# Mixed key pairs of the maxima spread over two items, with the size taken between two exponentials

## The chip, the cores and the metric

The program runs on one core of one Trainium2 chip. The metric is the device time of one execution in microseconds (us), lower being better. The kernel before took 14402.4 us as the median of three runs (14353.14, 14402.4 and 14412.16 us).

The engines are named as the profile names them: PE is TensorE's matmul, PEld its weight load, ACT ScalarE, DVE VectorE, POOL GpSimd, SP SyncE (here only a queue of DMAs).

## The reference, cut to what matters

There are N = 3327 nodes with 128 features. The first layer is a graph layer with residual and layer norm. The second, which takes nearly all the time, is an attention with 128 heads of 8 components each over all nodes, with the adjacency matrix added to the scores twice:

```python
q = (x @ Wq.T).reshape(d, n, h)          # d = 128 heads, n = 3327 nodes, h = 8
k = (x @ Wk.T).reshape(d, n, h)
v = (x @ Wv.T).reshape(d, n, h)
a = jnp.einsum('dnh,dmh->dnm', q, k) * scale
a = a + spatial_encoding + edge_encoding  # both are adj
a = jax.nn.softmax(a, axis=2)
out = jnp.einsum('dnm,dmh->dnh', a, v)
out = out.reshape(n, h * d)
return out @ Wo.T
```

So 128 matrices of 3327 x 3327 scores are made, and of each row its maximum, the exponentials less that maximum, their sum and their product with v.

The adjacency matrix is sparse, with at most 16 entries used in a row. The kernel therefore computes the dense part without it and adds each node's neighbours in a separate pass; the two are joined at the end.

## The kernel before, in words

**Stages.** Up to 460 us the first layer is computed. Up to about 890 us the queries, keys and values are projected and written to DRAM, the queries and keys split into three bf16 parts each, whose products are put together by stacking 48 rows (`KR`). From then to about 14,150 us the attention runs, and then the last stage joins, normalizes and projects.

**The sums.** The heads are worked on in 32 groups of four (`GH`). For each group the queries come in seven blocks (`BLOCKS`): six of 512 and a last one of 255. For each block a loop over 26 tiles of 128 keys (`t`) makes, for each head, the transposed scores in a PSUM bank `e_ps` (L620, three banks), the exponentials `es` (L630), and, two tiles later, the products with v (L588, function `products`). A step over one `t` has two halves of two heads each. In the last block one bank holds two heads of 255 columns (`per = 2`).

**The maxima.** The exponentials need each query's maximum over the keys. The same scores are made a second time, queries on the partitions, 76 items ahead of the sums. An item (`max_products`, L441) fills two PSUM banks `m` (L447; there are two such pairs) with 1024 keys of one head, and VectorE takes the maximum (L466). For 128 queries and four heads there are 13 items: three for each head, and one for the last 255 keys of all four. A full block has 52 items and 52 halves, so one item goes with each half; in the last block one item goes with each `t`. [...]

**Mixed pairs.** For two heads in four (`MIXED`), the first item's 1024 keys are stored as half sums and half differences of neighbouring keys, 512 of each, since max(a, b) = (a + b)/2 + |a - b|/2. Here ScalarE takes the absolute value of the differences' bank (`size`, L458), and one custom VectorE instruction (L461) adds it to the sums' bank and takes the maximum of 512 instead of 1024. Both banks belong to one item; in ScalarE's queue `size` stands ahead of both exponentials of its half. These keys are made by `mixed_keys` (L252) in the projection stage, are stored in `kk_d`, and are loaded by `load_group` into rows 64 and up of `k_st`.

**What sets the order.** Each engine's queue is in the order in which the Python code emits it. The maxima come from a generator (`maxima`, L375) that the loop over `t` advances between its own matmuls. After a block's maxima, `lowest` (one turn later) reduces them, and `to_queries` (eight turns after that) transposes them and sends them over DRAM into the row of `q_st` that makes the matmul subtract the maximum (L431, L435). All of these DMAs, the loads of groups (L326, issued when the maxima reach block 3 of the group before) and of queries, the stores of results and the traffic of the neighbours' pass are issued in order on SyncE's one queue.

**The neighbours.** A second generator, `beside`, is advanced once in four `t` (`PACE`). It first sorts keys and values by node in 256 steps (`by_node`), then takes 26 tiles of nodes (`neighbours`, L480), mostly on GpSimd: 16 steps for the scores of the neighbours, the maximum over the 16 slots on VectorE (`top`, L534), the exponentials on ScalarE, and 16 steps for the values; 36 steps a tile.

## Time and profile before

| | us |
|---|---|
| median of the runs shown | 14402.4 |
| the profiled execution's own time | 14479.67 |
| its span, first to last instruction | 14478.0 |
| TensorE matmul busy | 13415.7 (93%) |
| ScalarE busy | 12902.2 (89%) |
| VectorE busy | 12606.3 (87%) |
| GpSimd busy | 5379.1 (37%) |
| exponentials L630, 21632 of them | 11403.2 |
| maxima L466, 9152 of them | 10662.9 |
| sizes L458, 1664 of them | 994.2 |

The profile is of one execution, taken by the hardware's profiler. Busy times of instructions that overlap are counted once, so that a group's busy time can be less than its count times its mean. Ends of matmuls are modelled. In the stretch from 12,000 to 12,500 us, which has no neighbours' pass, TensorE is busy for 490.5 us, ScalarE for 481.9 and VectorE for 460.9 of 500.

The chain that ended last is followed back from the last instruction, at each step to what released it; its shares say what the end waited for. An idle time of an engine is put down to the instruction that released it. Times in the timeline are from the span's start.

### The profile page before, as it was taken

How to read it: one execution, taken by the hardware profiler on the slowest of the kernel's cores; microseconds unless marked ns; L12 is line 12 of the kernel's file. 1: busy time of each engine (PE TensorE's matmuls, PEld its weight loads, DVE VectorE, ACT ScalarE, POOL GpSimd, SP SyncE). 2: the span in 40 equal slices, each digit the busy share in tenths (PEclk: the TensorE clock that was granted, in tenths of full speed). 3: DMA queues.
4: the chain of work that ended last, by engine and by line, in shares of the span. 5: the costliest groups of instructions: out<-in, count | busy, mean ns of one | idle time of the engine just before them, and what ended most of it. 6: DMA issues, size and time to landing. Idle time of an engine off the chain costs nothing.

```text
span 14478.0 us, 319633 instructions
## 1 busy us (share of the span) xinstructions
PE 13415.7 (93%) x131844; PEld 3272.9 (23%) x131844; DVE 12606.3 (87%) x14091; ACT 12902.2 (89%) x24068; POOL 5379.1 (37%) x4580
## 2 busy tenths in 40 slices
PE   8559999999998999999999999999989999999995
PEld 3212222222222222222222222222212222222213
DVE  6669999999998999898998899899988889999976
ACT  8539999999998999899999999999989989999982
POOL 0410000006665556565565556655646630000002
PEclk9769999999999999999999999999999999999996
DMA  6963333333454444444445544444344531100103
GB/s 252 160 99 32 29 30 31 30 30 77 73 72 62 72 68 75 69 77 74 69 68 68 73 72 72 76 74 71 68 62 75 73 48 18 18 16 11 19 5 101
DMA packets 2711814, 930.03 MB, mean 64 GB/s; under 512 B 2431635, under 2 KB 2559762, under 8 KB 2703683
## 3 DMA queue, kind: packets, MB, share of 16 engines
q1 hardware_dynamic: 2582147, 411.27, 27.7%
q0 software_dynamic: 124176, 453.33, 11.3%
q10 hardware_dynamic: 4016, 44.88, 0.9%
q8 instruction: 1034, 16.94, 0.5%
q14 instruction: 441, 3.61, 0.1%
HBM read 786.20 MB, written 151.91 MB: 65 GB/s over the span
## 4 chain that ended last, share of the span: by engine, by line
PE 72%; ACT 15%; DVE 4%; issue 3%; DMA 3%; POOL 2%; SPq 1%; another core or an unknown queue 0%; ACTq 0%; DVEq 0%; POOLq 0%
PE o L588 34%; PE m L447 29%; ACT es L630 9%; PE e_ps L620 8%; ACT size L458 5%; DVE mx L466 1%; DMA k_st<-k_d 1%; DVE top L534 1%; POOL more L699 1%; ACT o_sb L597 1%; DVE top_at L153 1%; PE acc L145 1%; DVE top_w L152 1%; DMA kk_d<-both_sb 0%; ACT unread L143 0%
## 5 line engine op out<-in xcount | busy, mean ns | idle before, releaser
L630 ACT ACTIVATE es<-e_ps 128x512 f32<-128x512 f32 x21632 | 11403.2, 604 | 515.4 <-PE e_ps L620 305.8
L466 DVE TENSOR_REDUCE mx<-m 128x1 f32<-128x1024 f32 (+1 forms) x9152 | 10662.9, 1215 | 615.5 <-PE e_ps L620 428.4
L620 PE MATMUL e_ps<-q_st,k_st 50*128 50x512 bf16 (+1 forms) x23296 | 6920.9, 370 | 389.5 <-ACT es L630 136.5
L447 PE MATMUL m<-k_st,q_st 48*128 48x512 bf16 (+1 forms) x23296 | 6623.2, 370 | 230.6 <-DMA q_st<-q_d 118.5
L588 PE MATMUL o<-es,v 128*9 128x256 f32 (+1 forms) x83456 | 6732.5, 394 | 15.9 <-issue 15.9
L421 POOL CAST two<-nm 128x16 bf16<-128x16 f32 (+1 forms) x224 | 43.7, 195 | 6805.6 <-DVE nm L415 6805.6
L447 PEld LDWEIGHTS <-q_st 48*128 48x128 bf16 x23296 | 1442.2, 94 | 4861.4 <-issue 4816.2
L588 PEld LDWEIGHTS o<-es,v 128*9 128x9 f32 x83456 | 1242.4, 88 | 4889.4 <-issue 4881.5
L461 DVE CUSTOM_DVE_ANT_0 larger<-size,m 128x512 f32<-128x512 f32 x1664 | 1143.3, 687 | 736.0 <-ACT size L458 732.5
L620 PEld LDWEIGHTS <-k_st 50*128 50x128 bf16 (+1 forms) x23296 | 1415.5, 96 | 695.1 <-issue 526.0
L458 ACT ACTIVATE size<-m 128x512 f32<-128x512 f32 x1664 | 994.2, 597 | 458.7 <-PE e_ps L620 308.3
L521 POOL TENSOR_TENSOR prod<-qn,near_rows 128x1024 f32<-128x1024 f32 x416 | 985.8, 2370 | 98.9 <-DMA near_rows<-kn_d,near 78.0
L557 POOL TENSOR_TENSOR acc<-acc,prod 128x1024 f32<-128x1024 f32 x390 | 885.0, 2269 | 30.6
L556 POOL TENSOR_TENSOR prod<-near_rows,s 128x1024 f32<-128x1024 f32 x390 | 772.0, 1980 | 11.8 <-DMA near_rows<-vn_d,near 4.8
L523 POOL TENSOR_TENSOR half<-prod 128x512 f32<-128x512 f32 x416 | 530.0, 1274 | 32.6
L490 POOL DMA_INDIRECT near_rows<-kn_d,near x416 | 417.3, 1003 | 109.5 <-issue 57.1
L490 POOL DMA_INDIRECT near_rows<-vn_d,near x416 | 411.8, 990 | 65.1 <-issue 25.0
L145 PE MATMUL acc<-a_t,x 128*128 128x512 f32 (+1 forms) x728 | 305.2, 581 | 65.6 <-DMA a_t<-in_adj_dram 44.1
L525 POOL TENSOR_TENSOR quarter<-half 128x256 f32<-128x256 f32 x416 | 254.5, 612 | 32.6
L540 POOL TENSOR_TENSOR s<-s,gain 128x2048 f32<-128x2048 f32 x26 | 93.8, 3608 | 349.7 <-ACT s L539 349.7
L699 POOL TENSOR_TENSOR more<-n_t,down 128x1152 f32<-128x1152 f32 (+1 forms) x26 | 101.0, 3884 | 276.0 <-ACT down L697 138.4
L145 PEld LDWEIGHTS acc<-a_t,x 128*128 128x128 f32 x728 | 141.2, 196 | 229.3 <-issue 182.5
(151 smaller groups left out, 3441.0 us busy)
## 6 DMA issues: line engine op xcount, KB each, us to landing
q_st<-q_d SPq DMA_DIRECT2D x2304, 32.0 KB
a_t<-in_adj_dram ACTq DMA_DIRECT2D x13, 1663.5 KB
a_t<-in_adj_dram SPq DMA_DIRECT2D x13, 1663.5 KB
a_t<-in_adjt_dram SPq DMA_DIRECT2D x13, 1663.5 KB
a_t<-in_adjt_dram ACTq DMA_DIRECT2D x13, 1663.5 KB
q_d<-wq_sb SPq DMA_DIRECT2D x26, 768.0 KB
k_d<-wk_sb SPq DMA_DIRECT2D x26, 768.0 KB
k_st<-k_d SPq DMA_DIRECT2D x32, 623.8 KB
```

Source lines behind the costliest of these rows:

```text
L145: nc.tensor.matmul(acc[:, b, :w], x0[:, t, :], a_t[:, n0 : n0 + w], start=t == 0, stop=t == NT - 1)
L447: nc.tensor.matmul(m[:, n * step : n * step + width], q[64 : 64 + KR, j, i * P : (i + 1) * P], k[64 : 64 + KR, j, c0 : c0 + width], start= ...
L458: nc.scalar.activation(size, m[:, :NB], AF.Abs)
L461: nc.vector.tensor_tensor_reduce(larger, size, m[:, NB:], scale=1.0, scalar=LOWEST, op0=ALU.add, op1=ALU.max, accum_out=dst)
L466: nc.vector.tensor_reduce(dst, src, axis=AX.X, op=ALU.max)
L490: nc.gpsimd.indirect_dma_start(rows.rearrange("p d h -> p (d h)"), None, table, bass.IndirectOffsetOnAxis(ap=near[:, t, i : i + 1], axis=0))
L521: nc.gpsimd.tensor_mul(prod, qn, kg)
L556: nc.gpsimd.tensor_mul(prod, vg, share)
L557: nc.gpsimd.tensor_add(acc[:, :, :H], acc[:, :, :H], prod)
L588: nc.tensor.matmul(o[32 * j : 32 * j + VW, c : c + w], v4[:pt, j, t, :], e[j][:pt, c : c + w], start=t == 0, stop=t == NT - 1,)
L620: nc.tensor.matmul(bank[:pt, j, :w], k[: KR + 2, j0 + j, t * P : t * P + pt], q[: KR + 2, j0 + j, :w], start=True, stop=True,)
L630: nc.scalar.activation(es[:pt, :, :w], bank[:pt, :, :w], AF.Exp, scale=2.0)
```

## The change

A mixed head's 1024 paired keys and its next 1024 plain keys are spread anew over items. Before, one item held differences and sums, and two items held plain keys. Now the item "size" holds the differences in its first bank and 512 plain keys in its second, the item "sums" holds the sums and 512 plain keys, and a third item 1024 plain keys as before. There are as many items, banks and matmuls as before. VectorE takes a maximum over 512 in the item "size", and in the item "sums" the custom instruction on the first bank and a maximum over 512 on the second. The size is kept in SBUF from one item to the next.

In ScalarE's queue the size now stands between the two exponentials of its half. The loop over `t` gives one item to one half with both its banks, and in the last block makes both banks of four heads together, one item beside them.

The maxima's tile `mx` has five slots for each head instead of four, in two fixed buffers that are filled with the lowest value once.

Paired keys begin at the first whole row of 128 of a head (`paired_from`), so that they are eight rows instead of nine. The keys ahead of that are loaded behind the pairs. `mixed_keys` writes pieces of 1, 2, 4 or 8 rows. `load_group` loads the plain heads whole, the mixed ones in up to four pieces: 33 DMAs for keys in place of 24 for each group (30 for the first group, whose first head begins at a whole row).

The neighbours' maximum over 16 slots, one reduction before, is made by five elementwise maxima in four steps, so that a tile has 40 steps instead of 36.

```diff
@@ -49,6 +49,13 @@
 LEAD = 38
 TURN = 8
 MIXED = (0, 2)
+PAIRED = MW
+SLOTS_MX = 5
+
+
+def paired_from(head):
+
+    return -head * N % D
 
 
 def bank_cuts(width):
@@ -263,13 +270,15 @@
                 for head in range(HEADS):
                     if head % GH not in MIXED:
                         continue
-                    r0 = max(head * N // D, t * P)
-                    r1 = min((head * N + MW - 1) // D + 1, (t + 1) * P)
-                    if r0 < r1:
+                    first = (head * N + paired_from(head)) // D
+                    r0, r1 = max(first, t * P), min(first + PAIRED // D, (t + 1) * P)
+                    while r0 < r1:
+                        n = 1 << (r1 - r0).bit_length() - 1
                         nc.sync.dma_start(
-                            kk_d[:, r0 * D // 2 : r1 * D // 2].rearrange("r (p c) -> p r c", p=r1 - r0),
-                            sb[r0 - t * P : r1 - t * P].rearrange("p s a h c -> p (s a h) c"),
+                            kk_d[:, r0 * D // 2 : (r0 + n) * D // 2].rearrange("r (p c) -> p r c", p=n),
+                            sb[r0 - t * P : r0 - t * P + n].rearrange("p s a h c -> p (s a h) c"),
                         )
+                        r0 += n
 
             for t in range(NT):
                 g = slice(t * P * D, (t + 1) * P * D)
@@ -328,19 +337,22 @@
             heads = k_d[:, g * GH * N : g * GH * N + GH * N]
             for slot, parts in KROWS:
                 src = heads[: H * parts].rearrange("r (j n) -> r j n", j=GH)
-                for base, n0 in ((0, 0), (64, MW)):
-                    r = base + H * slot
-                    nc.sync.dma_start(k[r : r + H * parts, :, n0:N], src[:, :, n0:])
+                nc.sync.dma_start(k[H * slot : H * slot + H * parts, :, :N], src)
+                rows = slice(64 + H * slot, 64 + H * slot + H * parts)
                 for j in range(GH):
                     if j not in MIXED:
-                        nc.sync.dma_start(k[r : r + H * parts, j, :MW], src[:, j, :MW])
+                        nc.sync.dma_start(k[rows, j, :N], src[:, j])
                         continue
-                    at = (g * GH + j) * N // 2
+                    n0 = paired_from(g * GH + j)
+                    at = ((g * GH + j) * N + n0) // 2
                     for s in range(2):
                         nc.sync.dma_start(
-                            k[r : r + H * parts, j, s * NB : (s + 1) * NB],
-                            kk_d[s * PARTS * H : s * PARTS * H + H * parts, at : at + NB],
+                            k[rows, j, s * PAIRED // 2 : (s + 1) * PAIRED // 2],
+                            kk_d[s * PARTS * H : s * PARTS * H + H * parts, at : at + PAIRED // 2],
                         )
+                    if n0:
+                        nc.sync.dma_start(k[rows, j, PAIRED : PAIRED + n0], src[:, j, :n0])
+                    nc.sync.dma_start(k[rows, j, PAIRED + n0 : N], src[:, j, PAIRED + n0 :])
             v4 = load.tile([P, GH, NT, VW], F32, name="v4")
             for j in range(GH):
                 at = (g * GH + j) * N
@@ -372,6 +384,25 @@
             return queries[g, b]
 
 
+        mxs = [fixed.tile([P, NB // P, GH, SLOTS_MX], F32, name=f"mx{i}") for i in range(2)]
+        for mx in mxs:
+            nc.vector.memset(mx, LOWEST)
+
+        def items_of(mx, i):
+
+
+            plain = {
+                j: [([(j, c)], [(j, c + NB)], "all", [mx[:, i, j, c // MW : c // MW + 1]]) for c in range(0, 3 * MW, MW)]
+                for j in range(GH)
+            }
+            for n, j in enumerate(MIXED):
+                at = lambda slot: mx[:, i, j, slot : slot + 1]
+                yield [(j, PAIRED // 2)], [(j, PAIRED)], "size", [at(1)]
+                yield [(j, 0)], [(j, PAIRED + NB)], "sums", [at(0), at(3)]
+                yield plain[j][2]
+                yield from plain[j + 1]
+            yield [(0, 3 * MW), (1, 3 * MW)], [(2, 3 * MW), (3, 3 * MW)], "tails", [mx[:, i, :, SLOTS_MX - 1]]
+
         def maxima():
             for g in range(NG):
                 for b, (n0, w) in enumerate(BLOCKS):
@@ -383,18 +414,14 @@
                         group_of(g + 1)
                     if b + 1 < len(BLOCKS) or g + 1 < NG:
                         queries_of(g + (b + 1) // len(BLOCKS), (b + 1) % len(BLOCKS))
-                    mx = work.tile([P, NB // P, GH, 4], F32, name="mx")
+                    mx = mxs[(g * len(BLOCKS) + b) % 2]
                     for i in range(ntl):
-                        for j in range(GH):
-                            for c in range(3):
-                                yield from turn()
-                                banks = [(j, c * MW), (j, c * MW + NB)]
-                                yield (k, q, i, banks, NB, mx[:, i, j, c : c + 1], c == 0 and j in MIXED)
-                        yield from turn()
-                        yield (k, q, i, [(j, 3 * MW) for j in range(GH)], N - 3 * MW, mx[:, i, :, 3], False)
+                        for item in items_of(mx, i):
+                            turn()
+                            yield (k, q, i, *item)
                     late.append([1, lowest, (g, b, q, mx)])
             for _ in range(TURN + 4):
-                yield from turn()
+                turn()
                 yield None
 
         late = []
@@ -406,7 +433,6 @@
             while late and late[0][0] < 0:
                 _, part, args = late.pop(0)
                 part(*args)
-            return ()
 
         def lowest(g, b, q, mx):
 
@@ -438,32 +464,38 @@
                 chunk.rearrange("a (j n) -> a j n", j=GH)[:, :, :w],
             )
 
-        def max_products(item):
-
-            k, q, i, cols, width, dst, mixed = item
+        sizes = []
+
+        def max_item(item):
+
+            k, q, i, *banks, kind, dst = item
             m = ps_m.tile([P, MW], F32, name="m")
-            step = MW // len(cols)
-            for n, (j, c0) in enumerate(cols[::-1] if mixed else cols):
-                nc.tensor.matmul(
-                    m[:, n * step : n * step + width],
-                    q[64 : 64 + KR, j, i * P : (i + 1) * P],
-                    k[64 : 64 + KR, j, c0 : c0 + width],
-                    start=True,
-                    stop=True,
-                )
-                if n == len(cols) // 2 - 1:
-                    yield
-            if mixed:
-                size = work.tile([P, NB], F32, name="size")
-                nc.scalar.activation(size, m[:, :NB], AF.Abs)
+            tail = N - 3 * MW
+            for n, bank in enumerate(banks):
+                width = NB if len(bank) == 1 else tail
+                for x, (j, c0) in enumerate(bank):
+                    at = n * NB + x * NB // 2
+                    nc.tensor.matmul(
+                        m[:, at : at + width],
+                        q[64 : 64 + KR, j, i * P : (i + 1) * P],
+                        k[64 : 64 + KR, j, c0 : c0 + width],
+                        start=True,
+                        stop=True,
+                    )
                 yield
+            if kind == "size":
+                sizes.append(work.tile([P, NB], F32, name="size"))
+                nc.scalar.activation(sizes[-1], m[:, :NB], AF.Abs)
+            yield
+            if kind == "sums":
                 larger = work.tile([P, NB], F32, name="larger")
                 nc.vector.tensor_tensor_reduce(
-                    larger, size, m[:, NB:], scale=1.0, scalar=LOWEST, op0=ALU.add, op1=ALU.max, accum_out=dst
+                    larger, sizes.pop(0), m[:, :NB], scale=1.0, scalar=LOWEST, op0=ALU.add, op1=ALU.max, accum_out=dst[0]
                 )
-            else:
-                src = m if len(cols) == 2 else m.rearrange("p (n c) -> p n c", c=step)[:, :, :width]
-                nc.vector.tensor_reduce(dst, src, axis=AX.X, op=ALU.max)
+            src = m if kind == "all" else m[:, NB:]
+            if kind == "tails":
+                src = m.rearrange("p (n c) -> p n c", n=GH)[:, :, :tail]
+            nc.vector.tensor_reduce(dst[-1], src, axis=AX.X, op=ALU.max)
             yield
 
         def by_node():
@@ -531,7 +563,15 @@
                 yield
                 acc = side.tile([P, HEADS, CW], F32, name="acc", bufs=2)
                 top = side.tile([P, HEADS], F32, name="top")
-                nc.vector.tensor_reduce(top, s.rearrange("p i d -> p d i"), axis=AX.X, op=ALU.max)
+                m8 = side.tile([P, SLOTS // 2, HEADS], F32, name="prod", bufs=2)
+                for i in (0, 4):
+                    nc.vector.tensor_max(m8[:, i : i + 4], s[:, i : i + 4], s[:, 8 + i : 12 + i])
+                    yield
+                nc.vector.tensor_max(m8[:, :4], m8[:, :4], m8[:, 4:])
+                yield
+                nc.vector.tensor_max(m8[:, :2], m8[:, :2], m8[:, 2:4])
+                nc.vector.tensor_max(top, m8[:, 0], m8[:, 1])
+                yield
                 nc.gpsimd.tensor_copy(acc[:, :, CW - 1], top)
                 nc.gpsimd.tensor_sub(s, s, top[:, None, :].to_broadcast([P, SLOTS, HEADS]))
                 yield
@@ -563,15 +603,14 @@
         beside = (x for stage in (by_node(), neighbours()) for x in stage)
         with tc.manual_schedule(engines={ENG.PE, ENG.Activation, ENG.DVE, ENG.Pool, ENG.SP}):
 
-            def run_items(n):
-                for _ in range(n):
-                    item = next(stream, None)
-                    if item is not None:
-                        yield from max_products(item)
-
-
-            for _ in run_items(2 * LEAD):
-                pass
+            def next_item():
+                item = next(stream, None)
+                return max_item(item) if item is not None else iter(())
+
+
+            for _ in range(2 * LEAD):
+                for _ in next_item():
+                    pass
             o = ps_o.tile([P, NB], F32, name="o")
             nc.vector.memset(o, 0.0)
             waiting = []
@@ -610,17 +649,17 @@
                     for t in range(NT):
                         pt = P if t < NT - 1 else P - (NP - N)
                         e = []
-                        for half in range(2):
-                            m = run_items(1 if per == 1 or half == 0 else 0)
+                        for j0 in range(0, GH, 2 * per):
+                            m = next_item()
                             banks = []
-                            for j0 in range(half * 2, half * 2 + 2, per):
+                            for y in range(2):
+                                next(m, None)
                                 bank = ps_e.tile([P, per, NB // per], F32, name="e_ps")
                                 for j in range(per):
-                                    next(m, None)
                                     nc.tensor.matmul(
                                         bank[:pt, j, :w],
-                                        k[: KR + 2, j0 + j, t * P : t * P + pt],
-                                        q[: KR + 2, j0 + j, :w],
+                                        k[: KR + 2, j0 + y * per + j, t * P : t * P + pt],
+                                        q[: KR + 2, j0 + y * per + j, :w],
                                         start=True,
                                         stop=True,
                                     )
@@ -629,9 +668,12 @@
                                 es = probs.tile([P, per, NB // per], F32, name="es")
                                 nc.scalar.activation(es[:pt, :, :w], bank[:pt, :, :w], AF.Exp, scale=2.0)
                                 e += [es[:, j, :] for j in range(per)]
+                                next(m, None)
                             for _ in m:
                                 pass
-                            products(total, half)
+                            products(total, j0 // 2)
+                        if per == 2:
+                            products(total, 1)
                         size = NB // 2 if 0 < t < NT - 1 else NB
                         waiting.append((total, (g, v4, t, pt, e, n0), [(c, min(size, w - c)) for c in range(0, w, size)]))
                         total += 1
```

## The prediction

> **What bounds the kernel now.** I read the page's busy shares and chain first: they say which engines fill the span and what each adds to its end.
>
> ```profile
> PE 13415.7 (93%) x131844; PEld 3272.9 (23%) x131844; DVE 12606.3 (87%) x14091; ACT 12902.2 (89%) x24068; POOL 5379.1 (37%) x4580
> ...
> PE 72%; ACT 15%; DVE 4%; issue 3%; DMA 3%; POOL 2%; SPq 1%; another core or an unknown queue 0%; ACTq 0%; DVEq 0%; POOLq 0%
> PE o L588 34%; PE m L447 29%; ACT es L630 9%; PE e_ps L620 8%; ACT size L458 5%; DVE mx L466 1%; DMA k_st<-k_d 1%; DVE top L534 1%; POOL more L699 1%; ACT o_sb L597 1%; DVE top_at L153 1%; PE acc L145 1%; DVE top_w L152 1%; DMA kk_d<-both_sb 0%; ACT unread L143 0%
> ```
>
> Three engines are nearly full, so shares decide nothing. The chain does: TensorE holds 72%, but `size` (L458) has 5% of it, some 730 us, though it is only 994 us of work. Next the groups, with shapes kept apart, for prices (busy and mean ns):
>
> ```profile
> L630 ACT ACTIVATE es<-e_ps 128x512 f32<-128x512 f32 x19200 | 10098.7, 604 | 417.3 <-PE e_ps L620 271.8 <-PE m L447 122.7 <-PE o L588 2.6
> L466 DVE TENSOR_REDUCE mx<-m 128x1 f32<-128x1024 f32 x8320 | 9719.5, 1216 | 579.2 <-PE e_ps L620 416.6 <-PE m L447 149.6 <-issue 2.0
> ...
> L461 DVE CUSTOM_DVE_ANT_0 larger<-size,m 128x512 f32<-128x512 f32 x1664 | 1143.3, 687 | 736.0 <-ACT size L458 732.5 <-issue 3.5
> ...
> L458 ACT ACTIVATE size<-m 128x512 f32<-128x512 f32 x1664 | 994.2, 597 | 458.7 <-PE e_ps L620 308.3 <-PE m L447 81.4 <-DMA q_st<-q_d 66.8
> ...
> L534 DVE TENSOR_REDUCE top<-s 128x128 f32<-128x2048 f32 x26 | 95.0, 3655 | 2.7 <-POOL s L527 2.7
> ```
>
> L461 is preceded by 736 us of VectorE idle time that waits for `size`. How a `size` reaches the end is seen in the timeline (start and length in us). First ScalarE alone:
>
> ```profile
> 6043.07 2.17 ACT L630 ACTIVATE es<-e_ps 128x512 f32<-128x512 f32 x4 [0.32 <-PE e_ps L620]
> 6045.43 0.60 ACT L458 ACTIVATE size<-m 128x512 f32<-128x512 f32 x1 [0.18 <-PE e_ps L620]
> ...
> 6053.50 0.60 ACT L458 ACTIVATE size<-m 128x512 f32<-128x512 f32 x1 [0.18 <-PE e_ps L620]
> ...
> 6060.48 0.60 ACT L458 ACTIVATE size<-m 128x512 f32<-128x512 f32 x1 [0.18 <-PE e_ps L620]
> ```
>
> From one `size` to the next are 8.07 and 6.98 us. Between them lie seven and six halves (a half is one maximum item, two `e_ps` banks, two exponentials, one set of `o` products). The difference, 8.07 - 6.98, is one undisturbed half: h = 1.09 us. What remains, 6.98 - 6 x 1.09, is what each `size` costs: 0.44 us. Then all engines there:
>
> ```profile
> 6044.79 0.39 PE L447 MATMUL m<-k_st,q_st 48*128 48x512 bf16 x1
> ...
> 6045.02 0.38 PE L620 MATMUL e_ps<-q_st,k_st 50*128 50x512 bf16 x1
> ...
> 6045.92 2.06 ACT L630 ACTIVATE es<-e_ps 128x512 f32<-128x512 f32 x4
> 6046.06 0.69 DVE L461 CUSTOM_DVE_ANT_0 larger<-size,m 128x512 f32<-128x512 f32 x1 [0.45 <-ACT size L458]
> ...
> 6046.56 0.37 PE L620 MATMUL e_ps<-q_st,k_st 50*128 50x512 bf16 x1
> 6046.67 1.22 DVE L466 TENSOR_REDUCE mx<-m 128x1 f32<-128x1024 f32 x1
> ```
>
> Take P = 6044.79 as the half's start. L458 is issued ahead of both exponentials, and runs from P+0.64 to P+1.24, after the second bank of `m` (P+0.23, 0.38 long). Each exponential in a closed row ends 0.49 later ((2.06 - 0.60) / 3), so the first ends at P+1.72. There are three `e_ps` banks; the second matmul of the next half reuses that exponential's bank. It would start at P + 1.09 + 0.23 = P+1.32 and starts at 6046.56, P+1.77: TensorE lost 0.45 us, the same number. The other waits that matter:
>
> ```profile
> DVE larger L461 <- ACT size L458: 732.5, 1643, 66.2
> ...
> POOL acc L535 <- DVE top L534: 490.6, 26, 57.0
> ...
> PE e_ps L620 <- DMA q_st<-negmax_d: 119.3, 6, 32.4
> ```
>
> The maximum L534 (3.66 us, 26 times) is 0.6% of the chain, 87 us. Six block starts wait for `negmax`. One is explained by SyncE's queue, where a store of 128x128 short pieces precedes a group load, which then needs 31 us for two issues:
>
> ```profile
> 4287.92 0.39 SPq L512 DMA_DIRECT2D near_d<-acc  x1
> 4288.36 31.09 SPq L333 DMA_DIRECT2D k_st<-k_d  x2
> ```
>
> [...]
>
> **The change part by part.**
>
> *Size between two exponentials.* ScalarE's order becomes es0, size, es1. The half before ends its last exponential at 6043.07 + 2.17 = P + 0.45, which is P' + 1.54 in its own half (P' = 6043.70); undisturbed, es0 so ends at P+1.05. Then size ends at P+1.54, es1 at P+2.03, the next half's es0 at P+2.52. es1 is what now queues behind size: its bank is needed two halves on, at P+2.18, and comes free at 2.03 + 0.05: in time. The next es0's bank is needed at 2 x 1.09 + 0.23 = P+2.41 and is free at P+2.57 (0.05 from an exponential's end to its bank's matmul, as at 6046.56). A stall of 0.16 is left; the following exponentials gain 1.09 - 0.98 = 0.11 a half and meet their banks. Unknown is whether that slack exists in every half: ends 0.05 (half of the jitter hidden) and 0.28. I take 0.17. Saved: 0.45 - 0.17 = 0.28. Of 1664 sizes, 12 fall before the main loop, and 24/26 x 1652 = 1525 in full blocks: -427 us.
>
> *VectorE.* The custom instruction now reads a `size` that ended at P+1.54, before its own bank is there (P+1.70): no wait. Per 13 items it had 11 reductions and 2 custom ones. A closed row of five reductions (6048.06, 5.74 us) gives 1.13 each, and the custom one takes 0.61 to the next start (6046.06 to 6046.67). A reduction over 512 isn't in the trace: 1.13 less 512 elements, which the pair 128x128 (L691, 278 ns) and 128x1152 (L704, 1345 ns) prices at 1.04 ns each, is 0.60; if nothing overlaps it is 0.68. I take 0.60. After: 9 x 1.13 + 2 x 0.60 + 2 x (0.61 + 0.60) = 13.8 us against 13 x 1.09 + 2 x 0.17 = 14.5 for TensorE. So it is hidden by TensorE; its lag after a sums item and four reductions is 0.12 + 4 x 0.04 = 0.28 us, and two `m` buffers allow about as much (a reduction's end to the matmul that needs its buffer). Cover gone, it costs 0 to 70 us; I take 0.
>
> *Last blocks (w = 255).* One item goes with four heads in one step. Sizes there lie 6.82 us apart (12126.18 to 12133.00) for six steps; after, 6 x 1.09 + 0.17 = 6.71. 832 steps / 6.5 x 0.11: -14 us, ends -40 and +20.
>
> *Top in five parts.* On 512, 512, 512, 256 and 128 elements[...] but in four places, 8 halves (9 us) apart. VectorE is idle some 0.4 us in 8 halves (14.5 - 13.8 over 13), so of each 0.6 to 0.7 between 0.2 and 0.6 stays: 20 to 62 us over 26 tiles, I take 40 against 87: -47. GpSimd waits longer (L535), four steps a tile: 256 + 26 x 40 = 1296 steps of four key tiles instead of 1192, 5184 of 5824. It ends earlier than the main loop by 640 x 2.2 us, so nothing is late but its own stores.
>
> *Group loads.* Each group's load has 33 key DMAs on SyncE instead of 24, the bytes alike. Behind them queue the values, the queries and the `negmax` of block 2. At the 31 places, from the issue of `q_st<-negmax_d` to the block's first `e_ps`, the timeline shows 1.5 to 13.9 us; 1.5 means stalled, and the mean margin above it is 5.3. Nine issues at 0.37 are 3.3 us more, and 0.5 is lost since the maxima lead by fewer us: summing what exceeds each margin gives 30 us. Lower end 0; upper end nine times 0.9 (22 us / 24), 8.1 us and 112 us. Taken: +30. Stores meet loads at other places than before (six waits, 119 us): 0, ends -60 and +60.
>
> *Rows of `kk_d`.* 66 writes instead of 67, 512 rows instead of 575: 0, ends -5 and +5. *Before the main loop* 76 items run at VectorE's pace and lose six pairs of waits for size: -8.
>
> Sum: -427 - 14 - 47 + 30 - 8 = -466 on the profiled execution's 14479.7: 14,014. That execution was 77 us over the median of the runs, 14402.4, so 13,937; I say 13,940 (-3.2%).
>
> **Rivals.** (a) VectorE becomes the bound: 0.68 for each 512 and 0.08 for the accumulator's read make 14.3 us per 13, and its lag exceeds two buffers by 0.2 in each six items: with swings, +70 to +140, 14,045. For it: 87% busy; against: 1.13 measured. (b) SyncE's loads: upper end and unlucky stores, +82 + 50: 14,070. (c) The change doesn't do what it says: size stalls TensorE by 0.45 in its new place (its wait ends later than P+1.05): +427, 14,365. Against: bank 2 is ready at P+0.61. (d) Slower: the load grows so long that every group change stalls. From 24 us more per load (twice the 22 of now) it decides: 31 x (24 - 5.3) = 580 eats all. At 26 it is 642 instead of 30: 14,550. For it: six stalls already; against: equal bytes. (e) The stall vanishes and stores miss: -260 - 60: 13,620 at most, 13,760 for half.
>
> **How the numbers follow.** Forecast 0.70, its own range 13,850 to 14,030; a 0.09, b 0.09, c 0.03, d 0.04, e 0.05. 13,820 to 14,130 leaves out c, d, most of e and the tails. About 0.5% (72 us) is what a measurement here can tell from none: faster 0.93, same 0.03 (c), slower 0.04 (d).
>
> **What would show it.** Sizes 7.8 and 6.7 us apart; L458 at about 2% of the chain; L461's wait gone; the second L620 two halves after a size 0.16 late; waits of L620 for `negmax` near 150 us. A wait of L447 for L466 of hundreds of us would mean (a); gaps of over 10 us at most group changes (d).

## The result, and the profile after

The changed kernel took 14149.58 us (median of four runs, 14142.6 to 14151.06) against 14381.56 us of the kernel before beside it (four runs, 14353.14 to 14412.16). The ratio is 0.9837, 95% interval 0.9812 to 0.9862. It is faster by 232 us (1.6%), half of what was forecast, and just above the range of 13,820 to 14,130.

The page of the profiled execution, busy shares and the chain by engine and line:

```profile
PE 13187.8 (93%) x131844; PEld 3737.8 (26%) x131844; DVE 12549.8 (89%) x15861; ACT 12888.5 (91%) x24068; POOL 5395.9 (38%) x4580
...
PE 62%; DVE 19%; ACT 8%; issue 5%; DMA 3%; SPq 1%; POOL 1%; another core or an unknown queue 0%; DVEq 0%; ACTq 0%; POOLq 0%
PE o L627 28%; PE m L478 28%; DVE mx L498 13%; PE e_ps L659 5%; ACT es L669 4%; ACT size L488 3%; DVE larger L492 3%; PE acc L152 1%; SPq L359 1%; POOL more L741 1%; DMA k_st<-k_d 1%; DVE top_at L160 1%; DVE top_w L159 1%; DMA k_d<-wk_sb 0%; DMA k_st<-kk_d 0%
```

ScalarE's share of the chain fell from 15% to 8% and `size` (now L488) from 5% to 3%, as meant. But VectorE rose from 4% to 19%, 13% of it at the maxima L498. The groups by form show where VectorE stands still:

```profile
L669 ACT ACTIVATE es<-e_ps 128x512 f32<-128x512 f32 x19200 | 10262.0, 611 | 477.6 <-PE e_ps L659 139.1 <-PE m L478 104.0 <-PE o L627 4.0
L498 DVE TENSOR_REDUCE mx<-m 128x1 f32<-128x1024 f32 x6656 | 7699.5, 1211 | 171.5 <-PE m L478 100.3 <-PE e_ps L659 64.7 <-PE o L627 1.3
...
L498 DVE TENSOR_REDUCE mx<-m 128x1 f32<-128x512 f32 x3328 | 2290.8, 688 | 948.0 <-ACT size L488 934.6 <-ACT es L669 11.5 <-issue 1.7
...
L492 DVE CUSTOM_DVE_ANT_0 larger<-size,m 128x512 f32<-128x512 f32 x1664 | 1126.0, 677 | 6.6 <-PE e_ps L659 5.2
```

The custom instruction (L492, before L461) has lost its idle time: 736.0 us then, 6.6 now. In its place the new maximum over 512 waits 934.6 us for ScalarE's `size`, although it doesn't use it. The waits, with the number of times and the longest:

```profile
DVE mx L498 <- ACT size L488: 934.6, 1615, 43.2
POOL acc L575 <- DVE top L573: 495.7, 23, 46.9
...
PE m L478 <- DVE mx L498: 166.8, 576, 1.2
...
PEld L659 <- DMA q_st<-negmax_d: 100.5, 10, 24.0
```

1615 of 1664 sizes have this wait. In the trace the maximum waits for the semaphore that ScalarE counts up at the end of each `size`, and none of the 1664 begins less than 0.03 us after its `size` has ended, so the wait comes from the order that the program sets. The timeline of ScalarE alone shows the sizes of one cycle of 13 items, and that of all engines shows one wait with the halves around it:

```profile
2062.25 0.59 ACT L488 ACTIVATE size<-m 128x512 f32<-128x512 f32 x1
2070.37 0.59 ACT L488 ACTIVATE size<-m 128x512 f32<-128x512 f32 x1
2077.28 0.59 ACT L488 ACTIVATE size<-m 128x512 f32<-128x512 f32 x1
```

```profile
2060.18 0.37 PE L478 MATMUL m<-k_st,q_st 48*128 48x512 bf16 x1
...
2061.31 0.37 PE L478 MATMUL m<-k_st,q_st 48*128 48x512 bf16 x1
...
2062.25 0.59 ACT L488 ACTIVATE size<-m 128x512 f32<-128x512 f32 x1
...
2062.44 0.37 PE L478 MATMUL m<-k_st,q_st 48*128 48x512 bf16 x1
...
2062.87 0.69 DVE L498 TENSOR_REDUCE mx<-m 128x1 f32<-128x512 f32 x1 [0.48 <-ACT size L488]
...
2063.48 0.68 DVE L492 CUSTOM_DVE_ANT_0 larger<-size,m 128x512 f32<-128x512 f32 x1
```

`size` ends at 2062.84 and the maximum begins 0.03 later, after 0.48 us of idling. The sizes are 8.12 and 6.91 us apart, 15.03 a cycle: before it was 8.07 + 6.98 = 15.05, forecast was 14.5. The plain halves begin 1.13 us apart (2060.18, 2061.31, 2062.44): VectorE's pace for a reduction of 1024, no longer TensorE's 1.09. With 13.8 us of work and two waits of 0.48, VectorE has 14.8 us of a cycle taken, and in this cycle it idles nowhere else. A full block (the median of them) went from 61.0 to 60.6 us; the forecast's 427 us over 192 full blocks meant 58.8.

### The profile page after: what moved, and what is told of

Same layout as the page of the kernel before. It is cut to its first block, busy times and chain, and to the rows that moved or that the text cites. A ratio compares the mean times of both kernels' runs of the same rounds, so it can differ in the third digit from the quotient of the medians.

```text
span 14147.1 us, 322831 instructions
## 1 busy us (share of the span) xinstructions
PE 13187.8 (93%) x131844; PEld 3737.8 (26%) x131844; DVE 12549.8 (89%) x15861; ACT 12888.5 (91%) x24068; POOL 5395.9 (38%) x4580
## 4 chain that ended last, share of the span: by engine, by line
PE 62%; DVE 19%; ACT 8%; issue 5%; DMA 3%; SPq 1%; POOL 1%; another core or an unknown queue 0%; DVEq 0%; ACTq 0%; POOLq 0%
PE o L627 28%; PE m L478 28%; DVE mx L498 13%; PE e_ps L659 5%; ACT es L669 4%; ACT size L488 3%; DVE larger L492 3%; PE acc L152 1%; SPq L359 1%; POOL more L741 1%; DMA k_st<-k_d 1%; DVE top_at L160 1%; DVE top_w L159 1%; DMA k_d<-wk_sb 0%; DMA k_st<-kk_d 0%
## 5 line engine op out<-in xcount | busy, mean ns | idle before, releaser
L669 ACT ACTIVATE es<-e_ps 128x512 f32<-128x512 f32 x21632 | 11566.9, 610 | 546.5 <-PE e_ps L659 172.8
L498 DVE TENSOR_REDUCE mx<-m 128x1 f32<-128x1024 f32 (+2 forms) x10816 | 10795.7, 1050 | 1131.0 <-ACT size L488 934.6
L478 PE MATMUL m<-k_st,q_st 48*128 48x512 bf16 (+1 forms) x23296 | 6444.1, 362 | 383.2 <-DVE mx L498 166.8
L659 PE MATMUL e_ps<-q_st,k_st 50*128 50x512 bf16 (+1 forms) x23296 | 6643.1, 367 | 154.9 <-DMA q_st<-negmax_d 97.5
L627 PE MATMUL o<-es,v 128*9 128x256 f32 (+1 forms) x83456 | 6650.7, 391 | 9.1 <-ACT o_sb L636 5.2
L478 PEld LDWEIGHTS <-q_st 48*128 48x128 bf16 x23296 | 1799.4, 93 | 4980.3 <-issue 4927.3
L447 POOL CAST two<-nm 128x16 bf16<-128x16 f32 (+1 forms) x224 | 44.1, 197 | 6433.4 <-DVE nm L441 6433.4
L492 DVE CUSTOM_DVE_ANT_0 larger<-size,m 128x512 f32<-128x512 f32 x1664 | 1126.0, 677 | 6.6 <-PE e_ps L659 5.2
L488 ACT ACTIVATE size<-m 128x512 f32<-128x512 f32 x1664 | 984.5, 592 | 136.1 <-DMA q_st<-q_d 58.2
```

The lines of the kernel that those rows point to most:

```text
L478: nc.tensor.matmul(m[:, at : at + width], q[64 : 64 + KR, j, i * P : (i + 1) * P], k[64 : 64 + KR, j, c0 : c0 + width], start=True, stop=True,
L488: nc.scalar.activation(sizes[-1], m[:, :NB], AF.Abs)
L492: nc.vector.tensor_tensor_reduce(larger, sizes.pop(0), m[:, :NB], scale=1.0, scalar=LOWEST, op0=ALU.add, op1=ALU.max, accum_out=dst[0])
L498: nc.vector.tensor_reduce(dst[-1], src, axis=AX.X, op=ALU.max)
L627: nc.tensor.matmul(o[32 * j : 32 * j + VW, c : c + w], v4[:pt, j, t, :], e[j][:pt, c : c + w], start=t == 0, stop=t == NT - 1,)
L659: nc.tensor.matmul(bank[:pt, j, :w], k[: KR + 2, j0 + y * per + j, t * P : t * P + pt], q[: KR + 2, j0 + y * per + j, :w], start=True, sto ...
```

## The experiments

Two theories of the small gain stood first. **W**: VectorE's wait for `size` is the loss. **V**: VectorE is the bound by its work alone, wait or not. Later runs take the other parts one by one. Unless another kernel is named, an edit is against the changed kernel.

### The size behind both exponentials

```diff
+            yield
             if kind == "size":
                 sizes.append(work.tile([P, NB], F32, name="size"))
                 nc.scalar.activation(sizes[-1], m[:, :NB], AF.Abs)
-            yield
```

> The changed kernel with one edit: the size stands behind both exponentials of its half instead of between them; the maximum over 512 of the same item is still issued behind it. Theory W (VectorE's maximum over 512 waits for the size, because both read one m tile, and VectorE with this wait sets the pace): the wait grows by one exponential, 0.49 us, twice in 13 items, so 0.98 on 15.03 us: some 3.9 us more in each full block of 60.6, about +800 us, near 14,950. Rival V (VectorE's own work of 13.8 us and the two m buffers set the pace, the wait fills idle time): within 50 us of 14,150.

Measured: 14905.09 us. The waits:

```profile
DVE mx L498 <- ACT size L489: 1724.7, 1643, 43.4
...
PE m L478 <- DVE mx L498: 1097.2, 2121, 1.2
```

No work was added to any engine; only the place of `size` in ScalarE's queue changed, to one exponential later. VectorE's wait grew by 790 us and the kernel's time by 755 over the 14149.58 above (one execution, on another chip). The wait is on the path almost one for one; W holds, V falls.

### The maximum ahead of the size, in two places

The maximum over 512 is emitted ahead of `size`, with `size` between the exponentials (the first run below) or behind both (the second, with the `yield` moved as above):

```diff
             if kind == "size":
+                nc.vector.tensor_reduce(dst[-1], m[:, NB:], axis=AX.X, op=ALU.max)
                 sizes.append(work.tile([P, NB], F32, name="size"))
                 nc.scalar.activation(sizes[-1], m[:, :NB], AF.Abs)
...
-            nc.vector.tensor_reduce(dst[-1], src, axis=AX.X, op=ALU.max)
+            if kind != "size":
+                nc.vector.tensor_reduce(dst[-1], src, axis=AX.X, op=ALU.max)
```

> The changed kernel with the maximum over 512 issued ahead of the size, which stays between the two exponentials. If the m tile makes whichever reader is issued second wait for the first, the size now waits for VectorE (to P+1.7 or so), holds up the second exponential behind it in ScalarE's queue, and both e_ps banks come late: about 0.9 us a size, cycles near 16.0 us for 13 items, full blocks of some 65 us, near 15,000 in all. If only VectorE waits for ScalarE and not the reverse, near 13,700.

Measured: 14828.57 us (one execution). The waits:

```profile
DVE larger L493 <- ACT size L489: 889.3, 1364, 1.8
ACT size L489 <- DVE mx L487: 826.9, 1594, 7.9
```

The wait has turned round: now `size` waits for the maximum (1594 times, about 0.52 us each), and holds the second exponential behind it in ScalarE's queue. The sums' instruction then waits for that later `size` as well (the first line). Whichever reader of the two banks is emitted second waits for the first (0.48 us in the changed kernel, 0.52 here), so the wait comes from the order of two readers of one tile `m`, and from nothing in either operation.

> The changed kernel with the maximum over 512 issued ahead of the size, and the size behind both exponentials, so that VectorE waits for TensorE alone and the size waits for VectorE. W: VectorE's idle 0.48 us per size item goes, but the sums item directly after must wait for the later size (P+2.03 instead of P+1.54), so it lags 0.3 us and two m buffers hide only part: a full block of about 59.6 us, total near 13,950. V: 14,150 within 50.

Measured: 14405.57 us (14390.26 to 14410.39), ratio 1.0031 (1.002 to 1.0042). This was a miss by 450 us. The waits:

```profile
DVE larger L493 <- PE o L629: 716.0, 1104, 2.3
...
DVE larger L493 <- ACT size L490: 350.7, 522, 1.9
ACT size L490 <- DVE mx L488: 326.6, 1314, 7.9
```

A later `size` gives the maximum time, but the sums' custom instruction, one item on, now comes before its `size` is done: 1626 waits of 0.66 us on average. The first line names PE, but each of these waits has the length of those for `size` (in the timeline 0.66 us with either name, ending as `size` ends): a wait for two semaphores is put down to the one that came last in the records. In one cycle the sizes lie 8.20 and 7.09 us apart. My estimate had looked at the first of the two waits alone.

### The sums one item later

To the second of these kernels one swap is added, which puts a plain item between `size` and sums:

```diff
                 yield [(j, PAIRED // 2)], [(j, PAIRED)], "size", [at(1)]
-                yield [(j, 0)], [(j, PAIRED + NB)], "sums", [at(0), at(3)]
                 yield plain[j][2]
+                yield [(j, 0)], [(j, PAIRED + NB)], "sums", [at(0), at(3)]
```

> As the run before (maximum first, size behind both exponentials), and the 1024-key item is put between the size item and the sums item, so that the sums item finds its size ready. W: only ScalarE's 0.16 us per size is left, 14.5 us per 13 items, a full block of 58.0 us, total near 13,620. V: 14,150 within 50.

Measured: 13958.89 us (13950.19 to 13963.96), ratio 0.9718 (0.9699 to 0.9736). It leaves out nothing of the reference and is faster than both kernels. ScalarE's sizes in the timeline:

```profile
2060.02 0.60 ACT L490 ACTIVATE size<-m 128x512 f32<-128x512 f32 x1
2066.76 0.60 ACT L490 ACTIVATE size<-m 128x512 f32<-128x512 f32 x1
2074.65 0.60 ACT L490 ACTIVATE size<-m 128x512 f32<-128x512 f32 x1
```

The cycle is 6.74 + 7.89 = 14.63 us, a full block 59.4. The expectation was too low by 340 us, mainly since it left out some 0.9 us at the edges of each block (59.4 less four cycles) and took 0.16 us for a stall that measures 0.20 to 0.26 (6.74 and 7.89 less six and seven halves of 1.09). The tile `m` still has its two readers here, but the list of waits has none of VectorE for `size`, and `size` waits for the maximum ahead of it 105 times, 109.4 us in all, against 1594 times and 826.9 us in the first run with the maximum ahead: the order between two readers cost little once the other had mostly been done long before.

### The size from elsewhere

Here `size` reads a fixed tile of zeros, so the two engines share no tile of PSUM. The differences of the paired keys are thereby left out of their maxima; the matmuls, the instructions and their places stay.

```diff
+        apart = fixed.tile([P, NB], F32, name="apart")
+        nc.vector.memset(apart, 0.0)
...
-                nc.scalar.activation(sizes[-1], m[:, :NB], AF.Abs)
+                nc.scalar.activation(sizes[-1], apart, AF.Abs)
```

> The changed kernel, but ScalarE takes the size of a constant tile in SBUF instead of the differences in m, so the pairs' maxima leave the differences out; every instruction, order and operand size stays, and only the shared m tile, which makes VectorE's maximum over 512 wait for the size, is gone. W: VectorE no longer idles 0.48 us per size item; 14.5 us per 13 items as the prediction had it, a full block of 58 to 59 us instead of 60.6, 1.6 to 2.6 us in 192 blocks and half in 32: 330 to 540 us below the changed kernel, 13,610 to 13,820. V: within 50 us of the changed kernel.

Measured: 13902.23 us (13895.06 to 13949.44), ratio 0.9648 (0.9613 to 0.9683). ScalarE's sizes:

```profile
2103.12 0.62 ACT L490 ACTIVATE size<-apart 128x512 f32<-128x512 f32 x1
2110.92 0.62 ACT L490 ACTIVATE size<-apart 128x512 f32<-128x512 f32 x1
2117.64 0.62 ACT L490 ACTIVATE size<-apart 128x512 f32<-128x512 f32 x1
```

They are 7.80 and 6.72 us apart, 14.52 a cycle, which are the forecast's own numbers (7.8, 6.7 and 14.5). The maximum's wait for `size` is gone; the sums' instruction waits for it 40 times, 16.1 us in all. A full block takes 59.0 us. So the rest of the arithmetic of the mixed pairs was right but for a little, and the wait is what it left out. The edit also frees `size` from waiting for its matmul, but in the changed kernel that wait stands in 7 places only, with 47.0 us. Two tiles of one bank each, in place of the shared one, weren't tried: the plain items' reduction runs over both banks as one tile.

### The changed kernel again, as the measure for these

> The changed kernel, unchanged, on the same chip as the run with the size from elsewhere: 0.984 of the kernel before, full blocks of 60.6 us. Its projection stage takes 428 us if the 29 us less than before belong to the change, and the same as in the other kernels of this chip if they belong to the chip.

Measured: 14201.04 us (14192.83 to 14235.82), ratio 0.9849 (0.9815 to 0.9884), on the same chip as the run before this one. The wait is thus worth 299 us, a little under the 330 to 540 that were expected of its removal.

### The top in five parts alone

The kernel before, with the five elementwise maxima and their steps in place of the one reduction:

```diff
-                nc.vector.tensor_reduce(top, s.rearrange("p i d -> p d i"), axis=AX.X, op=ALU.max)
+                m8 = side.tile([P, SLOTS // 2, HEADS], F32, name="prod", bufs=2)
+                for i in (0, 4):
+                    nc.vector.tensor_max(m8[:, i : i + 4], s[:, i : i + 4], s[:, 8 + i : 12 + i])
+                    yield
...
+                nc.vector.tensor_max(m8[:, :2], m8[:, :2], m8[:, 2:4])
+                nc.vector.tensor_max(top, m8[:, 0], m8[:, 1])
+                yield
```

> The kernel before with the neighbours' maximum in five parts and nothing else. As predicted: -47 us, 14,335. Rival C (each stall of over 3 us also halves TensorE's clock for 3.4 us or more, which the trace shows behind most of the 26 reductions, so their price was larger than the reductions): -100 to -150 us, near 14,255, and half-clock time in the main loop down from 539 us to under 300.

Measured: 14275.65 us (14224.83 to 14283.72), ratio 0.9926 (0.9901 to 0.9952), against 14359.59 us: 84 us, interval 69 to 142, where 47 were forecast.

### The changed kernel with the old top

The same edit undone in the changed kernel.

> The changed kernel with the neighbours' maximum as one reduction again. As in the run with the five parts alone, which moved by 84 us: 14,150 + 84 = 14,234. If a VectorE that sets the pace has no slack for it, more: its own 26 x 3.6 us and the halved clocks, up to +130. The prediction's own term would be +47.

Measured: 14304.56 us (14298.8 to 14311.7), ratio 0.9943 (0.9926 to 0.996). Without the five parts, mixed pairs, rows and loads together bring 80 to 100 us (by the ratio, or by the two medians, 14404.74 less 14304.56). Set against the whole change run again (0.9849 against 0.9943, or 14201.04 against 14304.56, each beside its own runs of before), the five parts then bring 104 to 135 us. That comparison of two chips is uncertain by about 55 us (the two intervals together), so it doesn't contradict the 84; both lie above 47. Chance may be part of the gap: the profiled run of the top alone, 14283.72 us, had its last full block at half clock (some 40 us, see the last section), the other one here had not, and the fastest run of the top alone took 14224.83.

### Where the top's gain comes from

In the windows of the kernel before around the reduction at 8366.40 (busy us of each engine, then TensorE's granted clock, DMA share and GB/s):

```profile
8364.00:8368.00 4.00, 3.99 (x48) 1.38 (x45) 4.00 (x4) 3.82 (x8) 0.00 (x0) 1.00 0.36 93
8368.00:8372.00 4.00, 0.78 (x8) 0.23 (x11) 4.00 (x3) 0.78 (x3) 1.89 (x2) 0.99 0.00 0
8372.00:8376.00 4.00, 4.00 (x37) 1.11 (x29) 2.66 (x5) 2.75 (x6) 2.90 (x1) 0.59 0.01 2
```

VectorE is held for 3.64 us, TensorE stands still for over 3 of 4 us (busy for 0.78), and then, fully busy, gets little more than half its clock (0.59). The stretches of full and of half clock in the trace's records begin on one grid of 3.41 us. 25 of the 26 reductions before are followed within 25 us by time at half clock, in stretches of about 3.4, 6.8 or 10.2 us, 143 us in sum. At 23 of the 26 the longest gap between matmuls is 2.35 to 3.38 us, less than one step of the grid, so half clock also followed where no step was idle throughout. And in 24 places a few us after the start of a block the clock falls with no gap longer than 0.59 us ahead of it, as here:

```profile
1326.80:1330.20 3.40, 2.71 (x20) 0.79 (x20) 3.31 (x6) 3.40 (x8) 0.39 (x2) 1.00 0.10 22
1330.20:1333.60 3.40, 3.40 (x22) 0.39 (x16) 1.92 (x2) 1.84 (x4) 0.00 (x0) 0.50 0.71 41
```

Laid on this grid, the main loop of before has 38 steps at full clock in which TensorE is busy for less than half, and half clock follows all of them; it follows 37 of the 239 that are busy for 50 to 90%, and none of the 3416 above that. In the changed kernel's trace it follows all 11 steps below half and none of the 3423 above 90%, and the other eleven traces have the same two outer limits. (The ends of matmuls are modelled, so these shares are estimates from the trace.)

With five parts (windows of the changed kernel that hold the first, the third and the last two of one tile, the same columns):

```profile
8344.00:8348.00 4.00, 3.81 (x44) 0.96 (x37) 3.51 (x7) 3.96 (x9) 0.00 (x0) 1.00 0.00 0
...
8364.00:8368.00 4.00, 3.42 (x36) 0.88 (x36) 4.00 (x6) 3.72 (x7) 0.00 (x0) 1.00 0.01 4
8376.00:8380.00 4.00, 3.37 (x44) 0.83 (x36) 3.88 (x9) 3.72 (x8) 3.07 (x2) 1.00 0.02 5
```

TensorE stands for at most 0.63 of 4 us here and keeps its clock. Over the main loop the clock records give 539 us at half clock before and 331 with the top alone (each with 95.6 us of one last block, see below), 328 with the change less the top and 184 with the whole change. A stall so costs itself and the half-clock stretch behind it: as an estimate, 87 us of the chain and at most half of 143, some 159 in all, of which the five parts won back 84 to 135. The two shares weren't measured apart.

### Rows and loads, and the pieces

The kernel before with `paired_from`, the new rows of `kk_d` and the new `load_group`:

```diff
-                    r0 = max(head * N // D, t * P)
-                    r1 = min((head * N + MW - 1) // D + 1, (t + 1) * P)
-                    if r0 < r1:
+                    first = (head * N + paired_from(head)) // D
+                    r0, r1 = max(first, t * P), min(first + PAIRED // D, (t + 1) * P)
+                    while r0 < r1:
+                        n = 1 << (r1 - r0).bit_length() - 1
...
```

> The kernel before with the paired keys beginning at whole rows, the writes in pieces of 1 to 8 rows and the new group loads, and nothing else. The prediction gave the writes 0 us and the loads +30, so +30. Theory R (the writes of eight rows instead of nine shorten the projection stage, as the changed kernel's main loop begins 27 us sooner, and the loads cost nothing that can be seen): projection stage 29 us shorter, total -25 us.

Measured: 14407.67 us, ratio 1.0004 (0.9995 to 1.0013). The 33 key DMAs in place of 24 cost nothing that can be measured: 3 us, at most 19, where 30 were forecast.

The kernel before with its nine rows, but written in pieces of 1, 2, 4 or 8:

```diff
-                    if r0 < r1:
+                    while r0 < r1:
+                        n = 1 << (r1 - r0).bit_length() - 1
...
+                        r0 += n
```

> The kernel before with its nine-row writes cut into pieces of eight and one row; bytes, keys and loads as before. If the shape of a write [...] shortened the stage, its 457 us fall by some 20. If the fewer rows did, it stays, or grows by up to 60 us since SyncE issues 67 DMAs more.

Measured: 14410.95 us, ratio 1.0006 (0.9989 to 1.0022). This run was made because the projection stage, from its first store to its last, took 456.8 us in the first trace and 427.4 in that of the changed kernel. With the pieces it took 455 us, so the shape of the writes didn't shorten it.

> The kernel before, unchanged, for a second profile. If the half clock for 95.6 us after the last maximum item belongs to the order of its instructions, it is there again, and the last full block takes about 97 us; if it depends on chance, the block takes 57 us. The block starts that wait for stores on SyncE's queue should be the same five, since queue order is fixed.

Measured: 14446.1 us in one execution, beside a median of 14404.74 (14383.06 to 14458.22, 29 runs). The last full block takes 96.9 us again. The same five blocks as in the first trace are over 15 us longer than the median of their like, as expected. The projection stage is treated in the last section.

## Why the prediction was half right

**The step that failed** is the sum for VectorE. It has no wait of the new maximum over 512 for `size`, as if ScalarE and VectorE could read the two banks of that item at once. That was my assumption and stood in no trace; no run here shows two such reads at once. The two banks are one tile with two readers, and the second emitted waits for the first: about 0.48 us on VectorE, in 1615 places, 934.6 us in all. Because of it the sum for VectorE, 13.8 us a cycle, was short by about 1, and "hidden by TensorE" no longer held. Of the 427 us for the full blocks there is left what 60.6 against 61.0 us gives in 192 blocks, some 77 us. The trace of before couldn't show such a wait, since its custom instruction reads `size` itself and so comes after it in any case.

**The rest of the same step** was right. With no shared tile the cycle is 14.52 us for 14.5, the spacings 7.80 and 6.72 for 7.8 and 6.7, and a full block of 59.0 us gives 384 of the 427. The price of a maximum over 512 is 0.61 us to the next start (2062.87 to 2063.48) for 0.60, the custom instruction's wait is gone, and a reduction of 1024 goes at 1.13.

**Rival (a)**, VectorE as the bound at 14,045, had the right engine and the right sign, "a wait of L447 for L466". Its mechanism, dearer maxima, was not it. The chain showed VectorE (19%) more plainly than that one wait, which has 166.8 us and not hundreds.

**The top** had the right cover and place but the wrong size: -47 for -84 alone, 104 to 135 within the change. The term "40 against 87" counted the reduction's share of the chain and put nothing down for the half clock that follows it (143 us). The durations were right: the five parts took 680 ns for each 512 elements, 413 for 256 and 292 for 128, so 2.75 us in four places, 0.69 in each, where 0.6 to 0.7 was taken.

**Loads and rows**: +30 and 0 were measured together as +3. The waits for `negmax`, forecast near 150 us, were 97.5 in ten places (119.3 in six before). Six blocks of before are over 10 us longer than the median of their like, 137 us in sum without the last full block; after there are five, 91 us. So (b) and (d) fall. The neighbours' pass with 40 steps ended some 1,400 us before the main loop, as worked out. **Rival (c)**, the old stall in a new place at 14,365, was near to what the mixing did without the top (14304.56): the cycle stayed at 15.03, but by another engine's wait. **Before the main loop**: the -8 isn't seen; on one chip the loop began at 1008.7 us in the kernel before and at 1009.4 in the changed kernel with the old top.

**The first two traces mislead in two places.** Their spans differ by 331 us, the medians by 232. Some 29 us are the projection stage and some 40 us the last full block, both below.

## What to carry to other kernels

In this program two engines that read different banks of one PSUM tile were put in order, whichever came first (0.48 us of waiting where ScalarE did, 0.52 where VectorE did). So before a read is moved, list the other readers of its tile, in the order of emission, and place each where the other is long done. A stall of TensorE is priced together with the half-clock stretch that follows it: here 25 of 26 stalls, most of them of 2.35 to 3.38 us, were followed by 143 us at half clock. The top done alone and undone within the change told what two whole profiles could not.

## What the runs showed unexpectedly

**One last block at half clock.** When the maxima have ended, one full block of sums is left, and the short one after it. In windows of the kernel before and of the changed one (columns as above):

```profile
14060.00:14080.00 20.00, 20.00 (x109) 2.65 (x108) 0.00 (x0) 11.52 (x22) 0.00 (x0) 0.50 0.00 1
14080.00:14100.00 20.00, 20.00 (x105) 2.65 (x102) 0.00 (x0) 10.96 (x21) 0.00 (x0) 0.50 0.00 1
```

```profile
13760.00:13780.00 20.00, 20.00 (x186) 4.24 (x182) 0.00 (x0) 19.71 (x38) 0.00 (x0) 1.00 0.01 2
13780.00:13800.00 20.00, 20.00 (x189) 4.24 (x188) 0.00 (x0) 20.00 (x38) 0.00 (x0) 1.00 0.01 2
```

The first stays at half clock for 95.6 us with TensorE always busy and takes some 97 us; the second takes 57.2. Both profiles of before and that of the top alone did so, the other traces not, rows and pieces included, which have the same order of instructions in that block. A sign of what decides it is in the records. All thirteen traces have one gap of 0.45 us between matmuls 2.8 us after the last maximum's matmul. In the three, the step of the clock's grid of 3.41 us in which the gap lies ends 1.67 to 1.92 us after the gap (1.69 in the first trace of before); in the other ten the steps end 0 to 1.04 or 2.17 to 3.29 us after it (3.22 in the first trace of the changed kernel). The grid itself lies at 2.40 us from the span's start in that trace of before and at 1.84 in that of the changed kernel. So chance, by where the grid lies, fits all thirteen, but it wasn't tested, and why the clock then stays at half for 95.6 us with TensorE busy is open. The slow block may also be part of the scatter of the kernel before (14338 to 14458 us); no run was made on that.

**A stage that differs by chip.** The projection stage took 427 to 429 us in the first trace of the changed kernel and in the four runs made on one chip (the size later, the second maximum first, the sums later, the top alone), and 445 to 457 in all other traces, seven of them on two other chips. (The record names no chip for the first traces of the two kernels.) The changed kernel itself stands in both sorts, with 427.4 and, again, 447.2. Packets of 4608 bytes on GpSimd's DMA queue took 353 to 361 ns on average in the short stages and 211 to 253 in the long ones. Why is open. Such a stage is compared on one chip alone.
